# Layer 3's attention with denominator runs of four slots, sums made by adding transfers, and the last tile's scores in quarters

## The chip, the cores and the metric

The kernel runs on one core of a Trainium2 chip. The metric is the device time of the whole kernel in microseconds, the median of several runs. The engines are named as in the profile: PE (TensorE, matmuls; PEld is its weight load), DVE (VectorE), ACT (ScalarE), POOL (GpSimd) and SP (SyncE, which here only issues transfers). A line number such as L1911 is a line of the kernel before.

## The reference

Four layers work on x, 2708 nodes of 256 features, with one adjacency matrix. Each layer adds a graph part and then a feed-forward part to x. Only layer 3 is touched:

```
def _L3_gnn_ref(H, A, W, a_l, a_r):                 # H = layernorm(x), A = adj
    mask = (A + eye) > 0
    Wh = (H @ W.T).reshape(n, HEADS, D_K)           # HEADS 4, D_K 64
    e = score_l[:, :, None] + score_r.T[None, :, :]
    e = jnp.where(e >= 0, e, NEG_SLOPE * e)         # NEG_SLOPE 0.2
    e = jnp.where(mask[:, None, :], e, -jnp.inf)
    alpha = jax.nn.softmax(e, axis=2)
    out = jnp.einsum('nhm,mhd->nhd', alpha, Wh).reshape(n, OUT_DIM)
    return jax.nn.elu(out)

def _L3_ffn_ref(x, weight, bias):
    return jnp.einsum('bsi,oi->bso', x, weight) + bias

x = x + _L3_gnn_ref(_layernorm(x), adj, L3_gnn_W, L3_gnn_a_l, L3_gnn_a_r)
x = x + _L3_ffn_ref(_layernorm(x)[None], L3_ffn_weight, L3_ffn_bias)[0]
```

Everything is in float32.

## The kernel before

x stays on the chip as `x`, 22 tiles of 128 nodes; the last tile, index FULL = 21, has LAST = 20 nodes. `mask` holds the adjacency as bytes. Layer 3's attention is done for the transposed result: for each tile j of source nodes and a range of target nodes, a matrix e of weights is made and multiplied from the left with the source tile's values `wh`.

**Turns and slots.** The target nodes are cut into three stretches of two halves: 512 + 512, 512 + 512 and 384 + 276. For each stretch the four heads are taken as two pairs. That gives six turns (m = 0 to 5), each with 22 slots, one for each j. The list `slots` holds all 132 in order. I call the turns 0 to 5; turn 4 and turn 5 are the narrow ones.

**One slot.** `make(n)` (L1902 to L1913) lets DVE make two e tiles (k = 0, 1 for the two heads of the pair), each by one SCALAR_TENSOR_TENSOR over both halves (L1911). It is called AHEAD = 2 slots ahead. Tiles come from the pool `ge` with 8 buffers; from turn 1 on every fifth comes from `more_e` with 2 more. Then PE does four matmuls for the numerator `num` (L1941): a 64-column part of the array for each head, one PSUM bank for each half. The denominator `den` (L1951) uses the same e with a column of `wh` spread over 32 columns, four matmuls side by side. Den's matmuls of two slots are held back and done together: a den run after each odd j. In the profile each of these float32 matmuls is two records, so a slot has 8 of num and 8 of den. For the last tile j = FULL, e is made like any other, with 20 of its rows in use; its two halves' num matmuls use different 32-row parts of the array, so all four can go side by side.

**Work between the slots.** After its matmuls each slot takes one step of every generator in `active`. In turn 0 that is `last_stretch` (the end of layer 2's feed-forward for the last nodes and their projection) and, at slot 19, `centred` (L245, L247). In turns 2 and 4, and a little into turns 3 and 5, it is `closing` (L1856 to L1891), once for each of the 16 finished node tiles of the stretch before; a new one starts every two or three slots. Its steps are: transpose the result (L1860, L1861); divide, and make the exponential for elu on ACT (L1864 to L1871); add elu to x in two DVE operations (L1873, L1874) and take the statistics (L1876, L1878, and two small ACT operations); two steps with nothing; transpose x (L213); multiply with the feed-forward weights (L260); form and store the output (L1889 to L1891). The third stretch is finished after the last slot by `close` and `last` (L1804 to L1839).

**Order.** From `begun` to the last slot, `in_order` keeps PE, DVE and ACT in the order in which the program is written. POOL and SP are not in that list. `rows_of` reads the next turn's rows into `slow` (SP transfers at slot 0, exponentials on ACT at slot 8). `slow` and `dT` lie in `arena`, whose last columns are unused in this stage; before it, `arena` holds the transposed input of layer 2's feed-forward until L367's last matmul. `behind` (L512) makes an instruction wait for a given transfer; `after` only fixes the order in a queue. `spread` names an operation in the middle of layer 2's attention.

Of the kernel before, what the change touches and what calls it, by code (L numbers as in the profile page):

```python
# [8 lines left out]
F32 = mybir.dt.float32  # L9
U8 = mybir.dt.uint8  # L10
I32 = mybir.dt.int32
AF = mybir.ActivationFunctionType
ALU = mybir.AluOpType
AX = mybir.AxisListType

P = 128
N = 2708
D = 256
DC = D // P
E = 8  # L20
NT = (N + P - 1) // P
W = 512
Q = P // 4

FULL, LAST = N // P, N % P
# [41 lines left out]
def adj_ffn4(ctx: ExitStack, tc: tile.TileContext, a: dict, out: bass.AP):  # L67
    nc = tc.nc
    v, s, g, te = nc.vector, nc.scalar, nc.gpsimd, nc.tensor

    const = ctx.enter_context(tc.tile_pool(name="const", reuse_waits="tile", bufs=1))
    work = ctx.enter_context(tc.tile_pool(name="work", reuse_waits="tile", bufs=3))
# [42 lines left out]
    def row_bc(pool, name, n, tag=None, into=None):  # L115

        ap = a[name]
        t = into
        if t is None:
            t = pool.tile([P, n], F32, name=name, tag=tag or name, bufs=None if tag else 1)  # L120
        g.dma_start(t, bass.AP(tensor=ap.tensor, offset=ap.offset, ap=[[0, P], [1, n]]))
        return t
# [24 lines left out]
    def after(i, past):  # L147

        tc.add_manual_dep(i.ins, past, mybir.DependencyInfo(
            mybir.DependencyClass.NoSync, mybir.DependencyReason.DATA), reason="order")  # L150
# [361 lines left out]
    def behind(i, past):  # L512
        for p in past:
            tc.add_manual_dep(i.ins, p.name, mybir.DependencyInfo(
                mybir.DependencyClass.Sync, mybir.DependencyReason.DATA), reason="scattered rows")
# [858 lines left out]
    with tc.tile_pool(name="t3", reuse_waits="tile", bufs=1) as t3:  # L1374
# [34 lines left out]
        with tc.tile_pool(name="g2", reuse_waits="tile", bufs=1) as gp:  # L1409
# [80 lines left out]
            p = ps_tmp()  # L1490
# [142 lines left out]
        def width(m):  # L1633
            return sum(q for _, q in turns[m][0])

        def rows_of(m, step):
            halves, pair = turns[m]
            n = (width(m) + P - 1) // P
            for k in range(2):
                dst = slow[:, m % 2, k, : n * P]  # L1640
                if step != "exp":
                    row_read(dst, kept3, 2 * pair + k, halves[0][0] // P, n)
                if step != "read":
                    lnexp(dst, dst, AF.Exp, scale=0.8)

        def factors(t0, t1):
            lnexp(G[:, t0:t1, :, 0], wh[:, t0:t1, :, DK], AF.Exp, scale=-0.8)
            lnexp(wh[:, t0:t1, :, DK], wh[:, t0:t1, :, DK], AF.Exp)
# [5 lines left out]
        with tc.tile_pool(name="h2", reuse_waits="tile", bufs=2) as hp:  # L1654
# [120 lines left out]
            for c0, w in parts:  # L1775
                own = tiles_of(c0, w)
                end = c0 + w == N
                hT, i = units(c0, w)
                if end:


                    pin(i.ins.name)
                    rows_of(0, "both")
                    factors(0, was[0][0][0])
                if was is not None:
                    at_once(finish(*was, end))
                y = ypool.tile([P, 4, D], F32, name="y", bufs=2)
                outputs(own, hT, y)
                if was is not None:
                    at_once(front(was[0]))  # L1790
                    for t in range(NT) if was[0][0][0] == 0 else ():
                        r = rows(t)
                        g.tensor_copy(mask[:, t, t * P : t * P + r], diag[:, t, :r])
                if end:
                    factors(was[0][0][0], own[0][0])
                was = (own, y)
        sums.close()

        with tc.tile_pool(name="g3e", reuse_waits="tile", bufs=1) as ge, ExitStack() as sums:
            psum_pool(sums, 2, 0)  # L1800
            wf = mat(ge, "L3_ffn_weightT", D)
            bf = row_bc(ge, "L3_ffn_bias", D, into=b_l1)

            def close(oT, hf, t, k, q):  # L1804

# [40 lines left out]
            def last_stretch():  # L1846

                own = was[0]
                yield from finish(*was, True)
                yield from front(own)  # L1850
                factors(own[0][0], own[-1][0] + 1)
                for t, _, _ in own:
                    scaled(t)
                    yield

            def closing(oT, hf, t, k, q):  # L1856

                p = ps_tmp()
                for pair in range(2):
                    te.transpose(p[:q, pair * P : (pair + 1) * P], oT[:, pair, hf, k : k + q], ident)  # L1860
                te.transpose(p[:q, D : D + P], dT[:, hf, k : k + q], ident)  # L1861
                yield
                rs = small.tile([P, NH], F32, name="rs4")
                v.reciprocal(rs[:q], p[:q, D : D + P].rearrange("p (h z) -> p h z", z=Q)[:, :, 0])  # L1864
                o = work.tile([P, D], F32, name="o")[:q]
                for h in range(NH):
                    s.activation(o[:, h * DK : (h + 1) * DK], p[:q, h * DK : (h + 1) * DK],
                                 AF.Copy, scale=rs[:q, h : h + 1])
                e = work.tile([P, D], F32, name="elu_e")[:q]
                s.activation(e, o, AF.Relu, scale=-1.0)  # L1870
                lnexp(e, e, AF.Exp, scale=-1.0)  # L1871
                yield
                v.scalar_tensor_tensor(x[:q, t, :], o, 0.0, x[:q, t, :], op0=ALU.max, op1=ALU.add)  # L1873
                v.scalar_tensor_tensor(x[:q, t, :], e, -1.0, x[:q, t, :], op0=ALU.add, op1=ALU.add)  # L1874
                st = small.tile([P, 6], F32, name="st")
                v.bn_stats(st[:q], x[:q, t, :])  # L1876
                mv = small.tile([P, 2], F32, name="mv1")
                v.bn_aggr(mv[:q], st[:q])  # L1878
                lnexp(mv[:q, 1:2], mv[:q, 1:2], AF.Ln, bias=eps[:q])
                lnexp(mv[:q, 1:2], mv[:q, 1:2], AF.Exp, scale=-0.5)  # L1880
                yield
                yield
                xT = gp.tile([P, DC, P], F32, name="xT3", bufs=3)
                turn_to(xT[:, :, :q], x[:q, t, :], q)
                yield
                p = times(xT, 0, q, wf, D)
                yield
                o = work.tile([P, D], F32, name="o")[:q]
                v.scalar_tensor_tensor(o, p, mv[:q, 1:2], bf[:q], op0=ALU.mult, op1=ALU.add)  # L1889
                v.tensor_tensor(o, o, x[:q, t, :], ALU.add)  # L1890
                nc.sync.dma_start(out[t * P : t * P + q, :], o)  # L1891

            def centred():
                centre(wf)
# [7 lines left out]
            def make(n):  # L1902

                m, j = slots[n]
                (c0, _), pair, w = turns[m][0][0], turns[m][1], width(m)
                scores[n] = []
                for k in range(2):
                    places[0] += 1
                    pool, bufs = ((more_e[0], 2) if more_e and places[0] % 5 == 0 else (ge, 8))
                    e = pool.tile([P, WIDE], F32, name="e", bufs=bufs)  # L1910
                    v.scalar_tensor_tensor(e[:, :w], slow[:, m % 2, k, :w], G[:, j, 2 * pair + k, :],  # L1911
                                           mask[:, j, c0 : c0 + w], op0=ALU.max, op1=ALU.mult)
                    scores[n].append(e)  # L1913
# [7 lines left out]
            for now, (m, j) in enumerate(slots):  # L1921
# [12 lines left out]
                if m == 0 and j + 4 < was[0][0][0]:  # L1934
                    scaled(j + 4)
                es = scores.pop(now)
                for hf, (h0, q) in enumerate(halves):
                    for k, e in enumerate(es):
                        some, at = ((slice(0, P), None) if j < FULL else
                                    (slice(hf * Q, hf * Q + LAST), (hf * Q, k * DK)))  # L1940
                        te.matmul(num[k * DK : (k + 1) * DK, hf, :q],  # L1941
                                  lhsT=wh[some, j, 2 * pair + k, :DK],
                                  rhs=e[some, h0 - c0 : h0 - c0 + q],
                                  start=(j == 0), stop=(j == NT - 1), tile_position=at)
                held.append((j, slice(0, P) if j < FULL else slice(2 * Q, 2 * Q + LAST), es))
                if j % 2 or j == NT - 1:
                    for i, some, es in held:
                        for hf, (h0, q) in enumerate(halves):
                            for k, e in enumerate(es):
                                z = Q * (2 * hf + k)  # L1950
                                te.matmul(den[z : z + Q, :q],  # L1951
                                          lhsT=wh[some, i, 2 * pair + k, DK : DK + 1]
                                          .to_broadcast([some.stop - some.start, Q]),
                                          rhs=e[some, h0 - c0 : h0 - c0 + q],
                                          start=(i == 0), stop=(i == NT - 1),
                                          tile_position=(some.start, z))
                    held = []
                while waiting and waiting[0][0] <= now:
                    active.append(waiting.pop(0)[1])
# [83 lines left out]
```

## Time and profile before

| What | Value |
|---|---|
| Median of 3 runs | 1908.99 us (1906.96 to 1911.32) |
| The profiled execution | 1918.45 us |
| Its span, first to last instruction | 1916.7 us, mean granted clock 0.983 |
| PE, share of the span | 95% |
| DVE / ACT / POOL | 57% / 34% / 18% |
| L1941 num, 1056 records | 215.8 us |
| L1951 den, 1056 records | 118.0 us |
| L1911 e, 264 operations | 287.0 us |
| Layer 3's slots | 1539.8 to 1898.9 us of the span |

The profile is of one execution on the chip. The span runs from the first to the last instruction. Ends of matmuls are modelled, so PE's time is best read from the start of one group to the start of the next. A busy share is a mean over stages; only the stage that the change touches matters here. Buffer numbers are left out of names; a name can be that of an older tile in the same place (`arena` for `slow` and `dT`, `L_gnn_b` for the bias `bf`).

### The profile page before, as it was taken

The page shows a single profiled execution, that of the slowest core. Times are in us where ns is not written, and L with a number is a line of the kernel's source. Part 1 is how long each engine was busy: PE and PEld are TensorE (multiplying, and loading weights), DVE is VectorE, ACT ScalarE, POOL GpSimd, SP SyncE. Part 2 cuts the span into 40 slices and gives each one's busy share as a digit, 9 for nine tenths or more (in the row PEclk, how much of TensorE's full clock was granted, in tenths as well). Part 3 has the DMA queues.
Part 4 walks back from the last instruction along what each step waited for, and adds up shares of the span by engine and source line. Part 5 has one row for each costly group of instructions (what it writes and reads, how often), then busy time and mean ns, then how long its engine had stood idle before and what let it go on. Part 6 is the DMA issues. An engine that isn't in the chain of part 4 may idle for free.

```text
span 1916.7 us, 25790 instructions
## 1 busy us (share of the span) xinstructions
PE 1826.6 (95%) x9453; PEld 1326.0 (69%) x9453; DVE 1097.8 (57%) x2498; ACT 642.8 (34%) x1459; POOL 344.1 (18%) x406
## 2 busy tenths in 40 slices
PE   7999998999999999999979799999899999999998
PEld 6888777888888888888778578888566632232344
DVE  6777862443433625354532265555355398999897
ACT  7868751222222303113222232222232551031131
POOL 1004254333322001303356300000000000000000
PEclk9999999999998999999989899999899999999999
DMA  8435656887773554544758410000101000000000
GB/s 276 139 109 161 219 187 223 318 331 279 279 284 107 178 150 121 142 105 136 211 161 319 141 50 1 1 1 1 44 1 34 17 1 23 23 12 28 20 20 16
DMA packets 88846, 233.33 MB, mean 122 GB/s; under 512 B 18015, under 2 KB 44679, under 8 KB 80648
## 3 DMA queue, kind: packets, MB, share of 16 engines
q1 hardware_dynamic: 71752, 189.18, 29.9%
q0 software_dynamic: 16960, 42.42, 7.0%
q8 instruction: 78, 1.28, 0.3%
q14 instruction: 56, 0.46, 0.1%
HBM read 216.29 MB, written 28.71 MB: 128 GB/s over the span
## 4 chain that ended last, share of the span: by engine, by line
PE 42%; DVE 2%; DMA 2%; ACT 2%; issue 1%; another core or an unknown queue 1%; POOL 0%; SPq 0%; POOLq 0%; DVEq 0%; ACTq 0%
PE num L1941 10%; PE ps_acc L1514 9%; PE den L1951 6%; PE ps_tmp L367 4%; PE ps_acc L1704 3%; PE yacc L719 3%; PE ps_tmp L260 2%; DMA L_ffn_beta<-in_L_ffn_beta 1%; PE ps_acc L670 1%; PE ps_acc L260 1%; PE ps_tmp L213 1%; DVE e L1911 1%; DVE e L1506 0%; ACT wh L1843 0%
## 5 line engine op out<-in xcount | busy, mean ns | idle before, releaser
L1911 DVE SCALAR_TENSOR_TENSOR e<-arena,G,mask 128x1024 f32<-128x1024 f32 (+1 forms) x264 | 287.0, 1149 | 13.6 <-PE den L1951 13.6
L1941 PE MATMUL num<-e,wh 128*64 128x512 f32 (+4 forms) x1056 | 215.8, 551 | 0.0
L1514 PE MATMUL ps_acc<-hh,e 128*128 128x257 f32 x882 | 199.2, 382 | 1.7 <-ACT o L1457 1.7
L1300 PE MATMUL acc<-sup,adrow 128*128 128x256 f32 x882 | 200.1, 384 | 0.4 <-DVE adrow L1268 0.4
L929 PE MATMUL acc<-msg,wt 128*128 128x256 f32 x882 | 198.6, 381 | 2.0 <-DVE wt L887 1.2
L1300 PEld LDWEIGHTS acc<-sup,adrow 128*128 128x128 f32 x882 | 166.0, 191 | 29.1 <-issue 5.6
L929 PEld LDWEIGHTS acc<-msg,wt 128*128 128x128 f32 x882 | 165.2, 190 | 28.4 <-issue 2.1
L1514 PEld LDWEIGHTS ps_acc<-hh,e 128*128 128x128 f32 x882 | 163.6, 190 | 29.2 <-ACT o L1457 4.3
L617 PE MATMUL yacc<-wb,hTs 128*128 128x256 f32 x736 | 170.6, 383 | 6.2 <-issue 3.4
L583 PE MATMUL ps_acc<-xTs,wa 128*128 128x256 f32 (+1 forms) x768 | 169.3, 373 | 5.8 <-DVE xTs L573 3.1
L585 ACT ACTIVATE hTs<-ps_acc,wa 128x256 f32<-128x256 f32 (+1 forms) x192 | 88.8, 465 | 247.1 <-PE yacc L617 164.5
L583 PEld LDWEIGHTS ps_acc<-xTs,wa 128*128 128x128 f32 x768 | 136.5, 190 | 32.1 <-DVE xTs L573 5.6
L617 PEld LDWEIGHTS yacc<-wb,hTs 128*128 128x128 f32 x736 | 138.3, 192 | 25.3 <-issue 3.8
L1941 PEld LDWEIGHTS num<-e,wh 128*64 128x64 f32 (+1 forms) x1056 | 66.5, 136 | 127.3 <-issue 105.6
L1506 DVE SCALAR_TENSOR_TENSOR e<-Rb,G,mask 128x640 f32<-128x640 f32 (+2 forms) x110 | 85.1, 774 | 90.5 <-PE ps_acc L1514 90.4
L1951 PE MATMUL den<-e,wh 128*32 128x512 f32 (+4 forms) x1056 | 118.0, 548 | 0.0
L214 ACT COPY xT<-ps_tmp 128x256 f32<-128x256 f32 x98 | 33.6, 365 | 235.9 <-PE ps_tmp L213 218.3
L1265 DVE TENSOR_SCALAR mask<-adrow 128x1024 uint8<-128x1024 f32 (+1 forms) x66 | 41.4, 627 | 123.2 <-DMA adrow<-in_adjT 122.8
L719 PE MATMUL yacc<-wb,hTs 128*128 128x256 f32 x384 | 88.7, 385 | 1.1 <-DMA wb<-in_L_ffn_Wdp 1.1
L887 DVE SCALAR_TENSOR_TENSOR wt<-adrow,wt 128x640 f32<-128x640 f32 (+3 forms) x67 | 71.1, 1063 | 27.5 <-ACT wt L141 19.8
L1951 PEld LDWEIGHTS den<-e,wh 128*32 128x32 f32 (+1 forms) x1056 | 30.2, 108 | 77.9 <-issue 73.8
L619 DVE TENSOR_TENSOR ys<-yacc,wb 128x256 f32<-128x256 f32 x46 | 19.5, 424 | 112.7 <-PE yacc L617 103.4
(457 smaller groups left out, 2618.7 us busy)
## 6 DMA issues: line engine op xcount, KB each, us to landing
adhalf<-in_adjT SPq DMA_DIRECT2D x42, 677.0 KB
wb<-in_L_ffn_W2p SPq DMA_DIRECT2D x24, 1152.0 KB
wb<-in_L_ffn_Wdp SPq DMA_DIRECT2D x24, 1152.0 KB
wa<-in_L_ffn_W1b SPq DMA_DIRECT2D x24, 1028.0 KB
adrow<-in_adjT SPq DMA_DIRECT2D x42, 512.0 KB
adrow<-in_adjT SPq DMA_DIRECT2D x42, 320.0 KB
adrow<-in_adjT SPq DMA_DIRECT2D x21, 576.0 KB
adrow<-in_adjT SPq DMA_DIRECT2D x21, 448.0 KB
```

The lines of the kernel that those rows point to most:

```text
L367: te.matmul(p[:, :w], lhsT=w1[:, c, f * P : (f + 1) * P], rhs=xnT[:, c, c0 : c0 + w], start=(c == 0), stop=(c == DC - 1))
L583: i = te.matmul(p[:, f % 2, : m * P], lhsT=w1[:, c, f * P : (f + 1) * P], rhs=xT[:, c, : m * P], start=(c == 0), stop=(c == DC - 1))
L585: s.activation(hT[:, f, : m * P], p[:, f % 2, : m * P], AF.Gelu, bias=bias[:, f : f + 1])
L617: te.matmul(q[:, k, :], lhsT=hT[:, f, k * P : (k + 1) * P], rhs=w2[:, f, :], start=(f == 0), stop=(f == HC - 1))
L719: te.matmul(q, lhsT=hT[:, f, :], rhs=w2[:, f, :], start=(f == 0), stop=(f == HC - 1))
L929: te.matmul(p[:q, n - pair[0], :], lhsT=wt[:, k : k + q], rhs=msg[:r, j, :], start=(j == 0 and n == pair[0]), stop=(j == FULL - 1 and n == ...
L1300: te.matmul(p[:q, n - pair[0], :], lhsT=ad[:, k : k + q], rhs=sup[:, jj, :], start=(jj == 0 and n == pair[0]), stop=(jj == FULL - 1 and n ...
L1506: i = v.scalar_tensor_tensor(e[:r, :w], Rb[:r, c0 : c0 + w], G[:r, j, :], mask[:r, j, c0 : c0 + w], op0=ALU.max, op1=ALU.mult)
L1514: te.matmul(p[:, : D + 1], lhsT=e[:, k : k + q], rhs=hh[:, j, :], start=(j == 0), stop=False)
L1911: v.scalar_tensor_tensor(e[:, :w], slow[:, m % 2, k, :w], G[:, j, 2 * pair + k, :], mask[:, j, c0 : c0 + w], op0=ALU.max, op1=ALU.mult)
L1941: te.matmul(num[k * DK : (k + 1) * DK, hf, :q], lhsT=wh[some, j, 2 * pair + k, :DK], rhs=e[some, h0 - c0 : h0 - c0 + q], start=(j == 0), s ...
L1951: te.matmul(den[z : z + Q, :q], lhsT=wh[some, i, 2 * pair + k, DK : DK + 1] .to_broadcast([some.stop - some.start, Q]), rhs=e[some, h0 - c ...
```

## The change

Three things change in layer 3.

First, den runs are held for four slots (three in turn 0) instead of two, and one is done at j = FULL.

Second, in `closing`, elu is formed in one DVE operation (max of o and e - 1) into o, and a GpSimd transfer adds o to x in place. Three steps later come the statistics. The output is formed in one DVE operation that uses x where it used the bias, and a second GpSimd transfer adds it to the rows of `out`. Those rows (the first 2048) are filled with the bias by one SP transfer, DRAM to DRAM, ordered after `spread`; each adding transfer to `out` waits for it.

Third, for j = FULL one e tile, as wide as the first half alone, holds four 32-row quarters, one for each half and head. ACT copies the quarters of `slow`; one DVE operation makes e from them with `G_last` (factors by quarter) and a `corner` (the mask by quarter, one for each stretch), which POOL prepares in `last_mask` and `last_factors`. Two corners lie in the free end of `arena`.

```diff
--- before.py
+++ after.py
@@ -1633,6 +1633,28 @@
         def width(m):
             return sum(q for _, q in turns[m][0])
 
+        def quarters(halves):
+
+            return [(2 * hf + k, hf, k, h0, q) for hf, (h0, q) in enumerate(halves) for k in range(2)]
+
+        free = arena[:, 4 * WIDE + 2 * W :].bitcast(U8)
+        corners = [free[:, n * W : (n + 1) * W] for n in range(2)]
+        corners.append(gp.tile([P, first], U8, name="corner"))
+        assert len(corners) == len(stretches)
+        G_last = gp.tile([P, 2], F32, name="G_last")
+
+        def last_mask():
+            for halves, corner in zip(stretches, corners):
+                g.memset(corner, 0)
+                for z, _, _, h0, q in quarters(halves):
+                    z *= Q
+                    g.tensor_copy(corner[z : z + LAST, :q], mask[z : z + LAST, FULL, h0 : h0 + q])
+
+        def last_factors():
+            for z in range(P // Q):
+                g.tensor_copy(G_last[z * Q : (z + 1) * Q, :],
+                              G[z * Q : (z + 1) * Q, FULL, z % 2 :: 2, 0])
+
         def rows_of(m, step):
             halves, pair = turns[m]
             n = (width(m) + P - 1) // P
@@ -1781,6 +1803,7 @@
 
                     pin(i.ins.name)
                     rows_of(0, "both")
+                    last_mask()
                     factors(0, was[0][0][0])
                 if was is not None:
                     at_once(finish(*was, end))
@@ -1800,6 +1823,11 @@
             psum_pool(sums, 2, 0)
             wf = mat(ge, "L3_ffn_weightT", D)
             bf = row_bc(ge, "L3_ffn_bias", D, into=b_l1)
+
+            ap, n = a["L3_ffn_bias"], stretches[-1][0][0]
+            filled = nc.sync.dma_start(out[:n, :], bass.AP(tensor=ap.tensor, offset=ap.offset,
+                                                           ap=[[0, n], [1, D]]))
+            after(filled, spread)
 
             def close(oT, hf, t, k, q):
 
@@ -1849,6 +1877,7 @@
                 yield from finish(*was, True)
                 yield from front(own)
                 factors(own[0][0], own[-1][0] + 1)
+                last_factors()
                 for t, _, _ in own:
                     scaled(t)
                     yield
@@ -1870,8 +1899,11 @@
                 s.activation(e, o, AF.Relu, scale=-1.0)
                 lnexp(e, e, AF.Exp, scale=-1.0)
                 yield
-                v.scalar_tensor_tensor(x[:q, t, :], o, 0.0, x[:q, t, :], op0=ALU.max, op1=ALU.add)
-                v.scalar_tensor_tensor(x[:q, t, :], e, -1.0, x[:q, t, :], op0=ALU.add, op1=ALU.add)
+                v.scalar_tensor_tensor(o, e, -1.0, o, op0=ALU.add, op1=ALU.max)
+                g.dma_start(x[:q, t, :], o, accum_op=ALU.add)
+                yield
+                yield
+                yield
                 st = small.tile([P, 6], F32, name="st")
                 v.bn_stats(st[:q], x[:q, t, :])
                 mv = small.tile([P, 2], F32, name="mv1")
@@ -1885,10 +1917,9 @@
                 yield
                 p = times(xT, 0, q, wf, D)
                 yield
-                o = work.tile([P, D], F32, name="o")[:q]
-                v.scalar_tensor_tensor(o, p, mv[:q, 1:2], bf[:q], op0=ALU.mult, op1=ALU.add)
-                v.tensor_tensor(o, o, x[:q, t, :], ALU.add)
-                nc.sync.dma_start(out[t * P : t * P + q, :], o)
+                o = work.tile([P, D], F32, name="xn")[:q]
+                v.scalar_tensor_tensor(o, p, mv[:q, 1:2], x[:q, t, :], op0=ALU.mult, op1=ALU.add)
+                behind(g.dma_start(out[t * P : t * P + q, :], o, accum_op=ALU.add), [filled.ins])
 
             def centred():
                 centre(wf)
@@ -1902,8 +1933,20 @@
             def make(n):
 
                 m, j = slots[n]
-                (c0, _), pair, w = turns[m][0][0], turns[m][1], width(m)
+                halves, pair = turns[m]
+                c0, w = halves[0][0], width(m)
                 scores[n] = []
+                if j == FULL:
+
+                    w = halves[0][1]
+                    e = ge.tile([P, WIDE], F32, name="e", bufs=8)[:, :w]
+                    for z, _, k, h0, _ in quarters(halves):
+                        z *= Q
+                        s.copy(e[z : z + Q], slow[z : z + Q, m % 2, k, h0 - c0 : h0 - c0 + w])
+                    v.scalar_tensor_tensor(e, e, G_last[:, pair : pair + 1], corners[m // 2][:, :w],
+                                           op0=ALU.max, op1=ALU.mult)
+                    scores[n] = e
+                    return
                 for k in range(2):
                     places[0] += 1
                     pool, bufs = ((more_e[0], 2) if more_e and places[0] % 5 == 0 else (ge, 8))
@@ -1934,26 +1977,22 @@
                 if m == 0 and j + 4 < was[0][0][0]:
                     scaled(j + 4)
                 es = scores.pop(now)
-                for hf, (h0, q) in enumerate(halves):
-                    for k, e in enumerate(es):
-                        some, at = ((slice(0, P), None) if j < FULL else
-                                    (slice(hf * Q, hf * Q + LAST), (hf * Q, k * DK)))
-                        te.matmul(num[k * DK : (k + 1) * DK, hf, :q],
-                                  lhsT=wh[some, j, 2 * pair + k, :DK],
-                                  rhs=e[some, h0 - c0 : h0 - c0 + q],
-                                  start=(j == 0), stop=(j == NT - 1), tile_position=at)
-                held.append((j, slice(0, P) if j < FULL else slice(2 * Q, 2 * Q + LAST), es))
-                if j % 2 or j == NT - 1:
-                    for i, some, es in held:
-                        for hf, (h0, q) in enumerate(halves):
-                            for k, e in enumerate(es):
-                                z = Q * (2 * hf + k)
-                                te.matmul(den[z : z + Q, :q],
-                                          lhsT=wh[some, i, 2 * pair + k, DK : DK + 1]
-                                          .to_broadcast([some.stop - some.start, Q]),
-                                          rhs=e[some, h0 - c0 : h0 - c0 + q],
-                                          start=(i == 0), stop=(i == NT - 1),
-                                          tile_position=(some.start, z))
+                for z, hf, k, h0, q in quarters(halves):
+                    some, at, e = ((slice(0, P), None, es[k][:, h0 - c0 :]) if j < FULL else
+                                   (slice(z * Q, z * Q + LAST), (z * Q, k * DK), es))
+                    te.matmul(num[k * DK : (k + 1) * DK, hf, :q], lhsT=wh[some, j, 2 * pair + k, :DK],
+                              rhs=e[some, :q], start=(j == 0), stop=(j == FULL), tile_position=at)
+                held.append((j, es))
+                if len(held) == (3 if m == 0 else 4) or j == FULL:
+                    for i, es in held:
+                        for z, hf, k, h0, q in quarters(halves):
+                            some, e = ((slice(0, P), es[k][:, h0 - c0 :]) if i < FULL else
+                                       (slice(z * Q, z * Q + LAST), es))
+                            te.matmul(den[z * Q : (z + 1) * Q, :q],
+                                      lhsT=wh[some, i, 2 * pair + k, DK : DK + 1]
+                                      .to_broadcast([some.stop - some.start, Q]),
+                                      rhs=e[some, :q], start=(i == 0), stop=(i == FULL),
+                                      tile_position=(some.start, z * Q))
                     held = []
                 while waiting and waiting[0][0] <= now:
                     active.append(waiting.pop(0)[1])
```

## The prediction

> **What bounds the kernel now.** The change touches only the last stage, layer 3's attention and what lies beside it (from 1539.8 us of the span on). Its six turns have 22 slots each, one slot per tile j. I first asked for the busy time of each engine in windows cut at the turns; turns 1, 2 and 4 stand for the rest. Columns: window, length, then busy us (instructions) of each engine, granted clock, DMA share, GB/s.
>
> ```profile
> core 0: us, PE busy (x) PEld busy (x) DVE busy (x) ACT busy (x) POOL busy (x), PEclk, DMA share, GB/s
> 1606.90:1666.20 59.30, 59.30 (x357) 15.77 (x354) 57.02 (x48) 4.13 (x6) 0.00 (x0) 1.00 0.07 19
> 1666.20:1741.00 74.80, 74.80 (x430) 24.83 (x426) 68.10 (x96) 25.85 (x80) 0.00 (x0) 1.00 0.08 22
> 1800.10:1856.00 55.90, 55.50 (x424) 26.17 (x422) 49.86 (x94) 24.06 (x79) 0.00 (x0) 1.00 0.05 16
> ```
>
> PE has no gap; DVE is nearly full as well; POOL and the DMA engines are close to empty. Which of PE and DVE waits for the other is in the waits (who waited for what: us in total, times, longest):
>
> ```profile
> PEld num L1941 <- DVE e L1911: 15.8, 27, 0.8
> DVE e L1911 <- PE den L1951: 13.6, 19, 1.9
> ```
>
> DVE waits for PE to free e buffers. The 15.8 us are weight loads, at most 0.8 each, most of them beside an earlier matmul that still runs. PE itself is late only where a run of num stretches: by 1.06 at 1556.08 in turn 0 (4.64 to the next start, against 3.58 below) and by 0.47 at 1829.50 in turn 4. So **PE's own order of work sets the end**, and DVE's time counts only if it makes PE late.
>
> The timeline of PE (start, us, engine, line, ...), read by differences of starts because ends are modelled:
>
> ```profile
> 1650.45 3.65 PE L1941 MATMUL num<-e,wh 128*64 128x512 f32 x16
> 1654.03 1.92 PE L1951 MATMUL den<-e,wh 128*32 128x512 f32 x16
> 1655.89 3.65 PE L1941 MATMUL num<-e,wh 128*64 128x512 f32 x16
> ...
> 1681.61 1.92 PE L1951 MATMUL den<-e,wh 128*32 128x512 f32 x16
> 1683.46 0.44 PE L213 MATMUL ps_tmp<-ident,x 128*128 128x128 f32 x2
> 1683.83 1.94 PE L1941 MATMUL num<-e,wh 128*64 128x512 f32 x8
> 1685.70 1.13 PE L260 MATMUL ps_tmp<-L_ffn_weightT,xT 128*128 128x256 f32 x4
> ```
>
> Two slots of num take 3.58 us (1650.45 to 1654.03), one slot alone 1.87 (1683.83 to 1685.70). Hence a slot costs 1.71 and each run ends with 0.16 that is paid per run, not per slot. Den for two slots takes 1.85; it streams four columns at once where num streams two, so half of num's 1.71 for each slot, 1.71 for two, leaves 0.14 per run (inferred: no den run of another length is there). The two transposes of L213 take 0.37 before a num and 0.22 before an L260, so 0.15 again. **A change of the kind of work on PE costs about 0.15 us.** The narrow turns give the same: num 1.26 for one slot and 2.37 for two, so 0.15.
>
> **What the Trainium skill says.** "TensorEngine Tiling (Array Packing)", Key Properties: changing the tiling mode, not just the tile, drains the TensorE. The shapes 128*64, 128*32 and 128*128 are three modes, and the trace agrees with 0.14 to 0.16 us per change. "DMA: Bandwidth & Descriptors", SWDGE vs HWDGE vs iDMA: adding in a transfer has to come from GpSimd; no run here shows one yet. "SBUF — State Buffer", Who interferes with whom: a DVE operation in a two-port mode (copy, cast, tensor_scalar) locks GpSimd's descriptor writing out; the DVE work here is SCALAR_TENSOR_TENSOR, not in that list, at 1.2 us per 1024 elements. The trace has no GpSimd transfer under it, so this is open.
>
> **The change, part by part.**
>
> *Runs of four.* Den ran after every second slot, 11 runs a turn; it will run after j = 3, 7, 11, 15, 19, 21, so 6 runs (turn 0 in threes: 8). Where nothing else stands in the slot, a dropped den run saves two changes (num to den and back); where closing work follows in the slot anyway, one. I counted the runs of work of one kind (num, den, closing) slot by slot. A closing starts in slots 1, 3, 6, 8, 11, 13, 16, 18 of turns 2 and 4; its PE work was in its steps 0, 4 and 5, and three more yields put it in steps 0, 7 and 8. Turn 1: 22 runs become 12. Turn 2: 45 become 37. Turn 3, with the last closings' tail: 25 become 19. Turns 4 and 5 as 2 and 3. Sum 10 + 8 + 6 + 8 + 6 = 38 changes, times 0.15 = **5.7 us off PE**.
>
> *Turn 0* has few buffers (8, against 10 later) and DVE's leftover work of layer 2. Walked by hand: den of slots 0 to 2 ends at 1547.8, slot 7 waits for its e until 1558.7 as now (about 1.0), slot 8 now waits as well, until 1562.3 (1.5), because no den run stands in front of it; the end of slot 11's work is 0.3 late, and the later runs regain it. I take 0.1 saved (-1.5 to +0.8).
>
> *Buffers.* A run of four holds 8 of 10 e buffers, so DVE may make slot j+5 only when den of slot j is done, 1.0 us into the den run. It makes a slot in 2.43 (34 instructions in 40.85 us, 1.2 each): slots j+5 to j+7 are ready at 3.4, 5.9 and 8.3; PE needs them at 5.3, 7.0 and 8.7. Free of charge, with 0.4 us to spare at the tightest. Between closings PE is slower by their work and the margin is wider.
>
> *Last tile in quarters.* PE has as many matmuls of the same shape, four at a time as before: nothing. DVE makes one e of half the width instead of two: 2 x 1.28 becomes about 0.75 (the 660-wide takes 0.90), so 1.8 us a turn off DVE. ACT gets four copies of 32 partitions, 0.58 each if as the 64x512 copy of L1975, 2.3 in all. They wait for a buffer that den in slot 19 frees 1.0 us into its run; copies end at 3.3, e at 4.1, PE needs it after den and slot 20 at 3.6 + 1.9 = 5.4. Behind them on ACT stand the closing activations of slots 19 and 20, whose readers on DVE come after the next two e (4.9 us). No cost, if ACT is in time; else up to 1 us a turn.
>
> *The sums.* Each closing's DVE work, from its timeline:
>
> ```profile
> 1692.52 0.42 DVE L1873 SCALAR_TENSOR_TENSOR x<-o,x 128x256 f32<-128x256 f32 x1 [1.75 <-ACT o L1867]
> 1693.42 0.42 DVE L1874 SCALAR_TENSOR_TENSOR x<-elu_e,x 128x256 f32<-128x256 f32 x1 [0.47 <-ACT elu_e L141]
> 1693.88 0.43 DVE L1876 BATCH_NORM_STATS2 st<-x 128x6 f32<-128x256 f32 x1
> ...
> 1696.83 0.48 DVE L1889 SCALAR_TENSOR_TENSOR o<-ps_tmp,mv,L_gnn_b 128x256 f32<-128x256 f32 x1
> 1697.34 0.42 DVE L1890 TENSOR_TENSOR o<-o,x 128x256 f32<-128x256 f32 x1
> ```
>
> One of L1873/L1874 and L1890 go: 0.42 + 0.42 for each of 16 tiles, 13.5 us off DVE. As PE is the bound this is worth nothing by itself; its cover is PE's own work, and it pays for the den run's hold on the buffers. In their place POOL issues 32 transfers, about 0.75 each:
>
> ```profile
> 1526.32 0.75 POOL L127 DMA_DIRECT2D L_ffn_weightT<-in_L_ffn_weightT  x1 [10.13 <-PE ps_acc L1704]
> ```
>
> 24 us on an engine with 0.00 busy in these turns. **The new wait** is bn_stats (L1876), in order on DVE, for x's transfer. Behind it are DVE's next e's, and PE waits for those. Length: 0.75 issue, then 2.0 + 128 KB/436 GB/s = 2.3, an estimate from the same DMA page (Anatomy of one DMA), so 3.1. In the DMA view of 1526 to 1535, the packets of L127's 256 KB end 2.8 us after the issue. An add reads both sides: I take 4, between 3 and 8. Three yields give three slots: 10 us in turn 2 (73.6/22 = 3.35 a slot), 7.5 in turn 4 (54.7/22 = 2.49), at least 7.3 and 5.4 if DVE does nothing but e's. Hidden. The output's transfer has no reader.
>
> *The rest.* SP's fill of out, 2 MB, runs while DMA is at 0 or 1 tenths; 7 to 20 us at 100 to 300 GB/s, and the first add to out comes at 1690. On SP it stands after the loads that end at 1131; behind it are the weights at 1352, and at the latest the row loads at 1540, needed at 1598. POOL's 12 mask copies (0.3 for 128x128, so 0.3 to 1.2 each for 20 rows of up to 512) start when the arena is free, about 1523, and end by 1538 at worst; L127's load moves behind them, and its reader L245 runs at 1601; the memset of sc at 1539.9 follows. Nothing, or 1 us at most. The final tail (L1808 to L1839, 18 us) stays.
>
> **Sum.** 5.7 + 0.1 = 5.8 us. The profiled execution took 1918.45 (span 1916.7 and 1.75 around it) and should become 1912.6, its span 1910.9. It was 9.5 above the median of the runs, 1909.0; the difference carries over: **1903.2**. A measurement tells about 0.2% (3.8 us) from no change.
>
> **Rivals.**
> *The add is slow (slower).* At bn_stats DVE then waits the remainder, and three slots can't pass in less than the transfer's time L. Turn 4 decides: (L/3 - 2.49) x 22 eats the 5.8 at L = 8.3 us. At L = 10 turn 4 loses 18.5, turn 2 nothing: 1909.0 + 12.7 = 1921.7. For it: no adding transfer is in the trace, and descriptors may be written slowly beside a busy DVE. Against: 2.8 us for twice the bytes. Chance 0.17.
> *The buffers bind (no change).* If e's take so much longer in a run that PE waits 0.23 us in each of the 25 full runs, the gain is gone: 1909. For it: the margin is only 0.4. Against: the margin comes from durations that hardly vary. Chance 0.10.
> *The change of mode isn't what costs.* If den's 0.14 belongs to its slots, half is saved: 1906. Chance 0.05; L213's 0.15 speaks against it.
>
> **How the numbers follow.** The forecast has 0.68, of which 0.10 falls within 0.2% (turn 0 or ACT's copies cost 2 us). Faster 0.58 + 0.05 from the last two rivals = 0.63; same 0.10 + 0.08 = 0.18; slower 0.17 + 0.02 = 0.19. The range, 1899 to 1911, takes in 2 us on either side of the forecast's terms, the spread of the runs (1906.96 to 1911.32) and the two middle rivals; it leaves out the slow add.
>
> **What would show it.** Right: in turn 1 five den runs of 32 and a num run of 32 at 7.0 us instead of 2 x 3.58; turn 1 shorter by 1.5, 2 and 4 by 1.2, 3 and 5 by 0.9; DVE with more idle before e, put down to den. Wrong: idle before bn_stats put down to a transfer, idle of PE before num put down to e, or num and den runs whose sum per turn is unchanged.

## The result, and the profile after

The changed kernel takes 1904.76 us (median of 22 runs, 1898.77 to 1909.21) against 1908.82 for the kernel before (22 runs). The ratio is **0.9975**, with a 95% interval of 0.9967 to 0.9984: 3.1 to 6.3 us faster. The forecast was 1903.2, 5.8 us faster.

The two profiled spans differ by more, 1916.7 to 1902.2. Most of that isn't the change: the first num of turn 0 stands at 1539.76 before and at 1529.16 after, and between 1537.0 and 1548.6 in the ten profiles of the experiments, five of which have the fill of `out` and five not. The forecast of 1912.6 for the profiled execution rested on the profile's distance from the median of the runs, and that did not carry over: it took 1903.94. The comparison below therefore uses **the stage**, from the first num of turn 0 to the first transpose of the tail (L1808 before, L1836 after). Each turn is counted from its first num to the next turn's; all from PE starts in the trace.

| Turn | 0 | 1 | 2 | 3 | 4 | 5 | Stage |
|---|---|---|---|---|---|---|---|
| Before | 67.19 | 59.24 | 73.09 | 60.83 | 55.73 | 43.01 | 359.09 |
| After | 67.23 | 58.71 | 70.95 | 61.12 | 53.88 | 43.37 | 355.27 |
| Difference | +0.04 | -0.53 | -2.14 | +0.29 | -1.85 | +0.36 | **-3.82** |

The tail behind the stage is the same, 17.88 and 17.80 us. The stage's 3.8 us lie inside the measured interval, so no other gain is needed to explain it.

In the fences from here on, line numbers are those of the kernel that ran. In the changed kernel L1954 makes e, L1983 is num, L1991 is den, L1902 forms o and L1903 is the transfer that adds o to x. The windows at turns 1, 2 and 4 of the changed kernel, with the columns as before (window, length, busy of PE, PEld, DVE, ACT, POOL):

```profile
1596.40:1655.10 58.70, 58.70 (x356) 17.70 (x352) 50.61 (x44) 6.70 (x10) 0.00 (x0) 1.00 0.06 15
1655.10:1726.10 71.00, 71.00 (x418) 24.06 (x414) 61.28 (x80) 25.57 (x77) 11.36 (x13) 1.00 0.23 39
1787.20:1841.10 53.90, 53.37 (x418) 25.52 (x414) 43.91 (x79) 24.57 (x78) 11.26 (x13) 1.00 0.24 34
```

PE still fills its turns, but for 0.4 us in turn 4, where it waits for ACT, and a wait in turn 1 that the modelled ends hide (below). Over the whole stage DVE's busy time fell from 323.6 to 299.6 us. That is the 24 us which the prediction took off it; the windows by turn can't be compared one by one, as the prediction's window of turn 2 reaches 1.7 us into turn 3 and DVE works ahead across turns. POOL's 11 us in turns 2 and 4 are the transfers that it issues. PE's timeline in turn 1:

```profile
1596.40 7.09 PE L1983 MATMUL num<-e,wh 128*64 128x512 f32 x32
1603.41 3.64 PE L1991 MATMUL den<-e,wh 128*32 128x512 f32 x32
1606.98 7.99 PE L1983 MATMUL num<-e,wh 128*64 128x512 f32 x32
1614.91 1.49 PE L1991 MATMUL den<-e,wh 128*32 128x512 f32 x12
```

Four slots of num take 7.01 us and four of den 3.57. With 1.85 for two slots of den that is 0.86 a slot and 0.13 a run. The share of den's time that belongs to the run, which could only be inferred before, is now measured. The second num run takes 7.93: here PE waited 0.9 us. DVE's timeline at the same place says for what:

```profile
1592.79 9.65 DVE L1954 SCALAR_TENSOR_TENSOR e<-arena,G,mask 128x1024 f32<-128x1024 f32 x8 [0.93 <-PE den L1991]
1604.53 2.48 DVE L1954 SCALAR_TENSOR_TENSOR e<-arena,G,mask 128x1024 f32<-128x1024 f32 x2 [2.08 <-PE den L1991]
```

DVE had made e's up to the first of slot 4's two and then stood 2.08 us, until den freed a buffer. The later e's of the run came later by that, and 0.9 us of it reached PE. The adding transfers, as POOL's timeline and the view of line L1903 have them:

```profile
1667.01 0.96 POOL L1903 DMA_DIRECT2D x<-o  x1 [92.71 <-DVE o L1902]
1672.17 0.86 POOL L1903 DMA_DIRECT2D x<-o  x1 [4.20 <-DVE o L1902]
```

```profile
DMA to landing us min/median/max: 2.6/2.6/3.4
```

An issue takes 0.86 us and the sum has landed after 2.6. No bn_stats waited for it.

### The profile page after: what moved, and what is told of

Read it like the earlier page. It is cut to its first block, busy times and chain, and to the rows that moved or that the text cites. A ratio compares the mean times of both kernels' runs of the same rounds, so it can differ in the third digit from the quotient of the medians.

```text
span 1902.2 us, 25837 instructions
## 1 busy us (share of the span) xinstructions
PE 1819.7 (96%) x9453; PEld 1330.0 (70%) x9453; DVE 1074.9 (57%) x2460; ACT 657.2 (35%) x1483; POOL 382.5 (20%) x457
## 4 chain that ended last, share of the span: by engine, by line
PE 39%; DMA 4%; DVE 3%; ACT 2%; issue 1%; POOL 1%; POOLq 0%; SPq 0%; DVEq 0%; ACTq 0%
PE num L1983 10%; PE ps_acc L1514 9%; PE den L1991 6%; PE ps_tmp L367 4%; PE ps_acc L1726 3%; PE ps_tmp L260 2%; DMA L_ffn_beta<-in_L_ffn_beta 1%; PE yacc L719 1%; PE ps_acc L260 1%; DMA names<-taken,b_ix 1%; PE ps_tmp L213 1%; DVE e L1954 1%; DMA given<-ys,names 1%; DMA wb<-in_L_ffn_Wdp 0%; DMA taken<-names,r_ix 0%
## 5 line engine op out<-in xcount | busy, mean ns | idle before, releaser
L1954 DVE SCALAR_TENSOR_TENSOR e<-arena,G,mask 128x1024 f32<-128x1024 f32 (+1 forms) x252 | 274.9, 1149 | 34.1 <-PE den L1991 33.2
L1983 PE MATMUL num<-e,wh 128*64 128x512 f32 (+4 forms) x1056 | 214.3, 549 | 0.3 <-DVE e L1954 0.2
L1983 PEld LDWEIGHTS num<-e,wh 128*64 128x64 f32 (+1 forms) x1056 | 70.3, 136 | 122.4 <-issue 106.0
L617 PEld LDWEIGHTS yacc<-wb,hTs 128*128 128x128 f32 x736 | 137.2, 190 | 17.6 <-DVE ys L619 0.2
L1991 PE MATMUL den<-e,wh 128*32 128x512 f32 (+4 forms) x1056 | 112.2, 545 | 0.0
L719 PEld LDWEIGHTS yacc<-wb,hTs 128*128 128x128 f32 x384 | 73.5, 196 | 19.5 <-DVE ys L720 6.7
L1991 PEld LDWEIGHTS den<-e,wh 128*32 128x32 f32 (+1 forms) x1056 | 33.1, 109 | 73.7 <-issue 69.6
```

What stands on the lines that cost most here:

```text
L617: te.matmul(q[:, k, :], lhsT=hT[:, f, k * P : (k + 1) * P], rhs=w2[:, f, :], start=(f == 0), stop=(f == HC - 1))
L719: te.matmul(q, lhsT=hT[:, f, :], rhs=w2[:, f, :], start=(f == 0), stop=(f == HC - 1))
L1983: te.matmul(num[k * DK : (k + 1) * DK, hf, :q], lhsT=wh[some, j, 2 * pair + k, :DK], rhs=e[some, :q], start=(j == 0), stop=(j == FULL), ti ...
L1991: te.matmul(den[z * Q : (z + 1) * Q, :q], lhsT=wh[some, i, 2 * pair + k, DK : DK + 1] .to_broadcast([some.stop - some.start, Q]), rhs=e[so ...
```

## The experiments

The result was near the forecast, so the question was which parts make it and whether each step of the sum holds. The theory: PE pays for each change of its kind of work, runs of four save 38 changes, and DVE's relief only pays for the longer hold on e's buffers. The rival: DVE's relief is the gain. All stages below are from one profile each; turns that an edit does not touch agree to 0.06 us between profiles, so differences of 0.1 can be read.

### Relief without runs, and runs without relief

```diff
-                if len(held) == (3 if m == 0 else 4) or j == FULL:
+                if len(held) == 2 or j == FULL:
```

> The stage is counted from the first num matmul of turn 0 to the first transpose of the tail (L1808 before, L1836 after): 359.09 us before, 355.27 after. Theory (PE pays about 0.15 us for each change of its kind of work, and runs of four save 38 of them): den runs of two bring 42 changes back, 6.3 us, and give back turn 1's wait of 0.9 for e; stage about 360.5 (359.5 to 361). Rival (what helps is that DVE has less to do, by the adding transfers and the quartered last tile, which are all still there): stage stays at 355.3.

Measured: stage **359.24**, ratio 1.0001 (0.999 to 1.0012). DVE's relief and the quarters gain nothing without the runs of four. The theory's figure of 360.5 was 1.3 too high.

To the kernel before:

```diff
-                if j % 2 or j == NT - 1:
+                if len(held) == (3 if m == 0 else 4) or j == NT - 1:
```

> The kernel before with nothing but den runs of four (three in turn 0). Theory: PE's order alone makes the gain; 40 changes fewer than before, 6.0 us, less 0.9 for turn 1's first buffers and up to 2 where a fuller DVE makes e late in turns 2 and 4: stage 353.5 to 356. Rival: without the relief of DVE the longer hold on e's buffers makes PE wait; stage 358 or more.

Measured: stage **360.36**, ratio 1.0012 (1.0003 to 1.002). The theory's range was missed by 4.4 us and the rival's figure was right: runs of four alone lose. Over the stage PE's busy time fell by 2.9 us, from 358.1 to 355.2, but its idle time grew by 4.2, from 0.9 to 5.1. Turn 2 took 74.70 in place of 73.09. The timelines of DVE and PE there, two lines each:

```profile
1687.10 2.48 DVE L1911 SCALAR_TENSOR_TENSOR e<-arena,G,mask 128x1024 f32<-128x1024 f32 x2 [0.42 <-PE den L1951]
1689.50 0.48 DVE L1889 SCALAR_TENSOR_TENSOR o<-ps_tmp,mv,L_gnn_b 128x256 f32<-128x256 f32 x1
```

```profile
1685.91 3.64 PE L1951 MATMUL den<-e,wh 128*32 128x512 f32 x32
1690.03 0.44 PE L213 MATMUL ps_tmp<-ident,x 128*128 128x128 f32 x2 [0.48 <-DVE o L1889]
```

What PE waited for in turns 2 to 4 (us, times, longest):

```profile
PE ps_tmp L213 <- DVE o L1889: 4.0, 7, 1.2
```

PE waits for DVE's output operation L1889, which reads a ps_tmp that the transpose needs. L1889 stands behind two e's, and those behind den. So it isn't num that waits for e, as the prediction's rival had it, but a closing's PSUM buffer. Two readings are left: the order on DVE, or simply too much DVE work.

### Order or amount

To the kernel with runs alone: make the e's after the closing's steps of a slot.

```diff
-                if now + AHEAD < len(slots):
-                    make(now + AHEAD)
                 if j == 0:
...
                     if next(steps, "end") == "end":
                         active.remove(steps)
+                if now + AHEAD < len(slots):
+                    make(now + AHEAD)
```

> The kernel before with runs of four (stage 360.36 as it stood), but in each slot the e's for two slots ahead are made after the closing's steps and not before them: DVE's operation that reads ps_tmp no longer stands behind an e that waits for den. No transfers, no quarters. Theory (the wait for ps_tmp is what took the gain): idle of PE before L213 falls from 4.0 us to under 1, stage 354 to 356.5. Rival (DVE's amount of work is the bound): stage stays at 359 to 361, the wait only moves to num.

Measured: stage **362.74**, ratio 1.0029 (1.0018 to 1.004). This is above both ranges. Idle before L213 put down to L1889 is gone, but turn 2 still takes 74.91. There weight loads for num now wait 4.8 us for e, and DVE waits only 0.4 for den. Turn 0, which has no closings, lost 1.5 us as well (68.76 for 67.21). So the remedy that my theory of the order promised failed. But the edit also takes away some of DVE's lead: it now makes a slot's e's only after steps that need PE's work of two slots before. The run therefore doesn't show that the amount of DVE work is what binds.

### How much of the relief is needed

The sums back on DVE in the changed kernel, with the old distances of the steps (the fill of out goes as well; the output keeps the tile name of the changed kernel):

```diff
-                v.scalar_tensor_tensor(o, e, -1.0, o, op0=ALU.add, op1=ALU.max)
-                g.dma_start(x[:q, t, :], o, accum_op=ALU.add)
-                yield
-                yield
-                yield
+                v.scalar_tensor_tensor(x[:q, t, :], o, 0.0, x[:q, t, :], op0=ALU.max, op1=ALU.add)
+                v.scalar_tensor_tensor(x[:q, t, :], e, -1.0, x[:q, t, :], op0=ALU.add, op1=ALU.add)
...
+                v.scalar_tensor_tensor(o, p, mv[:q, 1:2], bf[:q], op0=ALU.mult, op1=ALU.add)
+                v.tensor_tensor(o, o, x[:q, t, :], ALU.add)
+                nc.sync.dma_start(out[t * P : t * P + q, :], o)
```

> The changed kernel with closing's sums back on DVE and its steps close together as before; runs of four and the quartered last tile stay. Theory: DVE takes back 16 x 0.85 us, which PE's work covers; stage 354.5 to 356.5, with about 1.1 us moved from turns 3 and 5 to turns 2 and 4. Rival: stage 358 or more, with PE idle before num put down to e.

Measured: stage **360.69**, ratio 1.0019 (1.0011 to 1.0028): the rival's side, though not with its sign. In turn 2 PE waited 2.1 us before L213 for DVE's output, as with runs alone, and not before num for e. And the same with the three yields kept, as an edit of that kernel:

```diff
                 v.scalar_tensor_tensor(x[:q, t, :], e, -1.0, x[:q, t, :], op0=ALU.add, op1=ALU.add)
+                yield
+                yield
+                yield
```

> The sums on DVE as in the run without transfers (stage 360.69), but with the three yields kept, so that the steps stand as far apart as in the changed kernel. Theory (DVE's 0.85 us per tile is what counts: with them the operation that frees ps_tmp, behind an e that waits for den, comes too late for PE's next L213): stage 359 to 361, idle before L213 put down to DVE's output operation remains. Rival (the spacing of the steps is what counts): stage 355 to 356.

Measured: stage **359.02** (the ratio, 1.0004 with 0.9992 to 1.0017, can't tell it from before). Taking the sums off DVE is worth 3.75 us with the steps at equal distances (359.02 to 355.27); with the sums on DVE the distances are worth 1.7 (360.69 to 359.02). The expected sign, idle before L213 put down to DVE's output, is there but small: 0.2 us in turn 2 and 0.4 in turn 4. PE waits more for ACT: 1.1 in each of these turns before the transpose of the result, for ACT's o, and 0.8 in turn 4 for ACT's xT. ACT's o in turn waits for a DVE operation, the reciprocal for the division.

The last tile whole again (two e's of full width, the old matmul positions), all else as changed:

```diff
-                if j == FULL:
...
-                    scores[n] = e
-                    return
...
-                                   (slice(z * Q, z * Q + LAST), (z * Q, k * DK), es))
+                                (slice(hf * Q, hf * Q + LAST), (hf * Q, k * DK)))
+                    e = es[k][:, h0 - c0 :]
...
-                                       (slice(z * Q, z * Q + LAST), es))
+                            some = slice(0, P) if i < FULL else slice(2 * Q, 2 * Q + LAST)
+                            e = es[k][:, h0 - c0 :]
```

> The changed kernel with the last tile's e made as before, two of full width; runs of four and the transfers stay. Theory: PE's matmuls are the same and DVE has 1.7 us more at each turn's end only: stage 355.3 to 356.5. Rival: the quarters are as needed as the transfers; stage 358 or more.

Measured: stage **356.32**; turn 1 takes 59.66 in place of 58.71, the others at most 0.09 more. The ratio, 0.9992 (0.9974 to 1.0011), can't tell it from before. The quarters are worth 1.05 us, nearly all in turn 1: there the first num run takes 7.97 without them and 7.01 with them, as DVE comes later to the e's of turn 1.

### Buffers

Shift the two spare e buffers so that both are in the first run of turn 1:

```diff
-                    pool, bufs = ((more_e[0], 2) if more_e and places[0] % 5 == 0 else (ge, 8))
+                    pool, bufs = ((more_e[0], 2) if more_e and places[0] % 5 == 2 else (ge, 8))
```

> The changed kernel with the places of the two spare e buffers shifted (places % 5 == 2 in place of 0), so that both stand ready in turn 1's first run. Theory: the wait of 0.90 us in turn 1 (num run of 7.92 us in place of 7.02) comes from the first run finding nine buffers, not ten; it goes, turn 1 takes 57.8, stage 354.4. Rival (DVE is late there because it starts turn 1 late, after the centring of the weights): turn 1 stays at 58.7.

Measured: turn 1 takes **57.81**, stage **354.37**, all other turns unchanged; ratio 0.9981 (0.9972 to 0.999), from other runs of before than the 0.9975 of the change, so those two don't rank the kernels. The 0.9 us are exactly the wait:

```profile
1604.03 10.85 DVE L1954 SCALAR_TENSOR_TENSOR e<-arena,G,mask 128x1024 f32<-128x1024 f32 x9 [0.93 <-PE den L1991]
```

```profile
1618.22 7.09 PE L1983 MATMUL num<-e,wh 128*64 128x512 f32 x32
```

DVE made nine in one go and not eight, and the second num run is 7.02 to the next start.

The other direction, no spare buffers at all:

```diff
-                    pool, bufs = ((more_e[0], 2) if more_e and places[0] % 5 == 0 else (ge, 8))
+                    pool, bufs = ge, 8
```

> The changed kernel with 8 e buffers in all turns, the two spare ones unused: a run of four holds all of them. Theory (who holds e's sets the pace): DVE makes a slot in 2.43 us and may start 1.0 us into the den run, so it ends slot j+7's e at 10.7 where PE wants it at 8.9; 1.9 us of wait for each full run in turns 1 and 3, 1.2 in turn 5, less in turns 2 and 4; turn 1 about 67 us, stage 372 to 385. Rival (two slots ahead is enough with any number of buffers): turn 1 at 58 to 60, stage under 358.

Measured: stage **403.53**, ratio 1.0238 (1.021 to 1.0266, two runs), above the range; turn 1 takes 66.29, near the 67 worked out. In turn 2 (87.22) part may be due to a lower granted clock, 0.95; turns 1 and 5 had 1.00. PE's timeline in turn 1 and DVE's wait there:

```profile
1632.99 9.19 PE L1983 MATMUL num<-e,wh 128*64 128x512 f32 x32
1642.11 3.64 PE L1991 MATMUL den<-e,wh 128*32 128x512 f32 x32
```

```profile
DVE e L1954 <- PE den L1991: 15.4, 5, 3.3
```

A num run takes 9.12 (1632.99 to 1642.11) in place of 7.02: 2.1 us of wait, where 1.9 was worked out. Turns 2 and 4 lost more than I expected; that the closings need DVE in the same time is a likely reason that no run tests.

Finally, runs of three in the kernel before, with nothing else:

```diff
-                if j % 2 or j == NT - 1:
+                if len(held) == 3 or j == NT - 1:
```

> The kernel before with runs of three in all turns, no transfers, no quarters. A run of three holds 6 of the 10 e buffers, so DVE can be two slots ahead while den runs, not one. Theory (runs of four alone lost because DVE stood idle for den while e buffers were held, 4.4 and 4.8 us in turns 2 and 4, and had no such room there): little idle for den in turns 2 and 4; 22 changes fewer in turns 1 to 5, 3.3 us; stage 355.8 to 357.5. Rival (an unrelieved DVE loses by any longer run): stage 359 or more.

Measured: stage **354.98**, ratio **0.9967** (0.9955 to 0.9978). DVE's waits in turn 2 (who waited for what: us, times, longest), of runs of four alone, then of runs of three alone:

```profile
DVE e L1911 <- PE den L1951: 4.4, 4, 1.8
```

```profile
DVE x L1873 <- ACT o L1867: 1.0, 2, 0.8
DVE x L1874 <- ACT elu_e L141: 0.9, 2, 0.5
DVE e L1911 <- PE den L1951: 0.9, 1, 0.9
```

The windows of turn 2 in the same order, with the columns as before:

```profile
1665.20:1739.80 74.60, 72.39 (x420) 24.90 (x418) 68.18 (x96) 24.49 (x78) 0.00 (x0) 1.00 0.07 22
1666.20:1738.70 72.50, 72.50 (x422) 24.74 (x418) 68.21 (x97) 25.27 (x79) 0.00 (x0) 1.00 0.07 23
```

The work of PE and of DVE is nearly the same in both. With fours PE also stands 2.2 us for DVE's output, and 72.39 + 2.2 is the whole turn; with threes PE has no gap. DVE stands 4.4 us for den with fours and 0.9 with threes. The two kernels differ in the length of the run alone, so that is what decides: it makes DVE idle, and a DVE that has little time over then comes late for PE. The runs show both ends of this; that each wait of PE goes back to DVE's idle at den is shown only at the place above. The stage came out 0.8 below the expected range, which I can't explain.

### The new wait without its cover

The three yields taken out of the changed kernel:

```diff
                 g.dma_start(x[:q, t, :], o, accum_op=ALU.add)
-                yield
-                yield
-                yield
```

> The changed kernel without the three yields between x's adding transfer and the statistics. It measures what the transfer costs where nothing covers it. Theory: DVE waits at each of the 16 bn_stats for the whole transfer, 2.6 us to landing by the profile[...]; DVE has about 11 us of room in turn 2 and 8 in turn 4, and what is over goes to PE: stage 375 to 390 in place of 355.3. Rival: the work behind bn_stats fills the gap anyway (PE lives on the e's made ahead): stage under 360.

Measured: stage **396.21**, ratio 1.0201 (1.0154 to 1.0248, two runs); turns 2 and 4 take 89.25 and 74.50, at a granted clock of 0.94 and 0.93, so part of the loss may be due to the clock. What DVE's statistics waited for:

```profile
  DMA x<-o: 47.2, 16
```

That is 2.95 us each, 0.35 more than the 2.6 to landing. DVE does wait for the whole transfer, as the theory had it, but the stage is longer than the 390 at most that it allowed.

## Why the prediction was right, and where its steps were off

- **PE's order sets the end, 0.15 us a change.** It held: 0.13 for den and 0.15 for num are now read from runs of four and two, and den's share belongs to the run, which rules out the rival that gave it to the slots. For a change from L260 to num it is 0.09 (1.06 against 0.97), so 0.15 for all 28 changes of turns 2 to 5 was a little high. Turns 2 and 3 together gave 1.85 for 2.1, turns 4 and 5 1.49 for 2.1: in turn 4 PE lost 0.49 before an L260, for ACT's xT, and 0.28 at an L213, where the kernel before had lost 0.47. What makes a change cost, a drain or something else, no run separates.
- **By turns.** I expected 2, 3, 4 and 5 shorter by 1.2, 0.9, 1.2 and 0.9. Turns 3 and 5 became longer, for the wider-spaced closings push one L213 and one L260, 1.2 us, over each turn's end; the text had counted them as changes and not as work. In the sum over two turns it cancels.
- **Turn 1, the term that was mis-sized:** -0.53 for -1.5. The step that failed is "a run of four holds 8 of 10 e buffers": the first run of turn 1 finds nine, because the spare two come by turns, every fifth tile. Moving them brought -0.90 and nothing else. This term is half of the difference between 5.8 and 3.8.
- **Turn 0** was given 0.1 saved; it lost 0.04.
- **"Free of charge ... between closings the margin is wider"** holds for the changed kernel only. For DVE's load of before it is false: runs of four alone lost 1.27. The remark that DVE's relief is worth nothing by itself and pays for the hold on the buffers was right, in numbers: relief alone +0.15, runs alone +1.27, both -3.82. It holds for runs of four; runs of three gained without any relief.
- **The last tile in quarters: nothing.** Off by 1.05 us, for DVE's shorter work at the end of turn 0 gives it a start in turn 1. Here the forecast had luck: without this gain, which it did not count on, the stage would have been shorter by 2.77 only, and turn 1 longer by 0.42.
- **The wait for x's transfer.** Taken as 4 us, from an estimate of 3.1 by the Trainium skill's page "DMA: Bandwidth & Descriptors" (Anatomy of one DMA); it took 2.6 to landing and 2.95 as DVE saw it without cover. Hidden, as forecast. The rival of a slow add needs 8.3 and is ruled out by that.
- **The rest.** The fill of out left SP at 1119.00 and moved data until about 1154, 35 us and not 7 to 20, with nothing waiting for it. POOL's copies of the mask took 0.5 to 0.7 each and were done at 1518.9. DVE waited 16.9 us for ACT's quarter copies, and the num runs just before the quarters were no longer for it (2.88 us in turn 1, 2.89 before).

Left open: what binds when the closings go first, and why the parts ahead of the stage differ by up to 20 us between profiles of the same work.

## What to carry to other kernels

Grouping work of one kind saves the changes between, but it holds buffers longer, and the engine that fills them can stand idle for them and then be late with everything behind it in its queue. So look for the bound engine's waits on all that other work, not only on the buffers. Try the length of a group before relieving the other engine: here groups of three, one number changed, gave a stage of 354.98 and a ratio of 0.9967, where groups of four needed transfers, a fill and a new layout of the last tile for 355.27 and 0.9975. The two aren't ranked by that, as their intervals overlap, and threes with the relief were not tried. Spare buffers that come by turns are not spare at once; count them for the first group.

## What was not expected of the hardware

A transfer from GpSimd that adds 128 KB into SBUF landed 2.6 us after its issue (3.1 for the one into DRAM), beside a DVE that was busy for 61 of 71 us. POOL's issue of one into SBUF took 0.85 to 1.24 us there, where the prediction took 0.75, so DVE's work did not hold it up by much. The plain copy of 256 KB in L127 took 2.8 to its last packet; size and end point differ, so this doesn't give the price of the adding itself. A transfer that fills 2 MB of DRAM from a repeated row took 35 us, which is some 60 GB/s.
